# First layer of a four-layer network: gates between the transpositions, 56 stationary columns, halved copies

## The chip, the cores and the metric

The kernel runs on one core of a Trainium2 chip. The core has TensorE (PE; its weight loads are shown as PEld), VectorE (DVE), ScalarE (ACT), GpSimd (POOL) and SyncE (SP), whose queue here issues nearly all DMAs. The metric is the device time of one execution in microseconds. Everything is float32.

## The reference

x has 8 images of 56 x 56 positions with 192 channels. Four layers follow each other, each of the form x = x + layer(group_norm(x)). Only the first is touched:

```python
p = silu(x @ p_w.T + p_b); q = silu(x @ q_w.T + q_b); v = silu(x @ v_w.T + v_b)   # 192 -> 576
a1 = rpe_mlp(positions, t1) * decay; a2 = rpe_mlp(positions, t2) * decay          # 112 x 576
qv = q * v
o1 = toeplitz(qv along w, a1); o2 = toeplitz(qv along h, a2)    # per channel, length 56
out = (p * (o1 + o2)) @ o_w.T + o_b                             # 576 -> 192
```

So for each of 576 channels, each row and each column of the image is convolved with a 56-long two-sided kernel of that channel. The second layer is an outlook attention, the third a windowed gated attention, the fourth a scan in four directions; they begin at about 2.1 ms and end the span.

## The kernel before

An image is kept with channels on partitions: `xa` has the first 128 channels of all 3136 positions, `xb` the last 64, with the image's two halves on the two partition halves. The 576 channels are nine sets of 64 (`NS`), worked in five chunks (`NC`): chunks 0 to 3 have two sets each, chunk 4, the tail, has one. Functions return lists of steps, and `merge(a, b)` calls two lists alternately. TensorE's order is the order in which the program calls (a manual schedule); the other engines' orders are chosen by the scheduler, and each engine works its queue in order.

The work on a chunk:

- `project(xn, c)`, four steps `g`: the q and v products for a band of 7 rows in each half of the image (L294 with `xa`, L301 with `xb`; two PSUM tiles, one for q and one for v; one in the tail), a Silu of each on ScalarE (L310), and the product q * v, written into `qv` twice: as it is (`straight`, L319, VectorE) and with the two image axes exchanged (`across`, L325, mostly GpSimd; in step 3 halved between GpSimd and VectorE). `qv` holds [channel, 56, 120]: one form in columns 0 to 55, the other in 64 to 119, reversed. There is one `qv`, so a chunk's products are written after the transpositions of the chunk before have read it.
- `turn_both(n)`, seven steps of 16 transpositions (L352), which bring positions onto partitions, and two copies of each PSUM tile (L357): rows 0 to 55 (`T2`) by VectorE into `ol`, rows 64 to 119 (`T1`) by ScalarE into `or`. In the tail this is `turn`, with four steps (L371, L378).
- `toeplitz(n)`: the other rows of `ol` and `or` are loaded with the Toeplitz matrices of set n: for image 0 from the small networks' output (L280, and stored to DRAM, L281), later from the stored tables (L275), on SP's queue, after the convolutions of set n - 2 have read their places.
- `convolve(n, ot)`, two steps per set of 32 matmuls (L395): one matmul per channel, contraction over 120 rows (56 of qv and table, a gap, 56 of table and qv), which gives o1 + o2 of that channel as 56 x 56. Two channels go side by side, to output rows 0 to 63 and 64 to 127. The stationary side takes 64 columns, that is the channel's 56 and 8 of the next one, so that the gap rows 56 to 63 of the output are written too. The PSUM tile is copied to `ot` as 120 rows at once: the first step of a set by VectorE (L415), the second by ScalarE (L413); in the tail two copies of 56 rows (L406).
- `post(c // 2, ...)` after chunks 1 and 3, seven groups: the gate p (L436, L443, Silu L450), the transposition of `ot`, with all 120 rows (L461), the product (L470), the output projection (L481, L486) and the addition to `acc` (L422, L424). `post_tail` does this for the tail (L526 to L572, L547 its transposition).

PSUM tiles of the first layer come from `banks()`, four buffers of two banks, handed out in turn; the inputs of the products, `s`, have four buffers too. The main loop takes, for each chunk c:

```python
merge(fill, turns)                      # post step of the chunk before, if any, with the turn
...
ahead = project(xn, c + 1) if two else project(nxt, 0) if more else []
...                                     # convs: the steps of convolve, toeplitz(m + 2) after each set
if c == NC - 2:
    ahead = [f for pair in zip(ahead, convs[0:4]) for f in pair]
    convs = convs[4:]
merge(ahead, beside)                    # the next chunk's projection, with norm steps beside it
for f in convs:
    f()
if c in (1, 3):
    fill = post(c // 2, xn, ot, acc)
```

`fill` is the post step in chunks 2 and 4, the tail's post step in chunk 0 of the next image, and empty in chunks 1 and 3 and in chunk 0 of image 0. `beside` holds, in chunks 0 and 1, the statistics of the finished image (`tell`, with small matmuls L98, table loads for the square root L128 and the VectorE operations L119 to L130 and L608), and in chunk 2 the normalization of the next one (`normalize`: L49 on VectorE, L595 on ScalarE).

Of the kernel before, what the change touches and what calls it, by code (L numbers as in the profile page):

```python
# [17 lines left out]
H = 56  # L18
# [38 lines left out]
def image_dma(queue, dram, xa, xb, store=False):  # L57


    parts = []  # L60
    for at in range(0, HW, HQ // 2):
        cols = slice(at, at + HQ // 2)
        parts.append((xa[0:CP, cols], dram[:, 0, cols]))
        parts.append((xa[CP:CA, cols], dram[0 : CA - CP, 1, cols]))
        h, own = at // HQ, slice(at % HQ, at % HQ + HQ // 2)
        parts.append((xb[h * CB : (h + 1) * CB, own], dram[CA - CP :, 1, cols]))
    for s, d in parts:
        if store:
            queue.dma_start(d, s)
        else:  # L70
            queue.dma_start(s, d)


def sub(ap, *dims):

    return bass.AP(ap.tensor, ap.offset, [list(ap.ap[0]), *(list(d) for d in dims)])
# [59 lines left out]
def layer0(cx, xin, xout, w, consts):  # L136
# [6 lines left out]
    tc, nc = cx.tc, cx.nc  # L143
    B = len(xin)
    NS, DS = 9, 64
    NC = 5
    NP = 112
    T2, T1 = slice(0, H), slice(64, 64 + H)
    cx.open(B)
    cx.between = ExitStack()  # L150
    with ExitStack() as es:
        gn = GroupNormSplit(cx, cx.between, w["gmat"])
        cp = es.enter_context(tc.tile_pool(name="l0c", bufs=1))
# [5 lines left out]
        def banks():  # L159
            return cx.tile(psc, [128, 2, 512], "c")  # L160
# [22 lines left out]
        with ExitStack() as pes:  # L183
# [22 lines left out]
            for t in (1, 2):  # L206
# [13 lines left out]
                for i in range(3):  # L220
                    ps = banks()[0:32, 0, 0:NP]
# [4 lines left out]
                for s in range(NS):  # L226
                    ps = banks()[0:DS, 0, 0:NP]
# [23 lines left out]
        qv = cx.tile(cp, [128, H, 120], "qv")  # L251
        nc.vector.memset(qv[:, :, H:64], 0.0)

        ND = DS * H
# [25 lines left out]

        def project(xn, c):

            n = 7 * H
            tail = c == NC - 1
            js = [2 * c] if tail else [2 * c, 2 * c + 1]

            def step(g):
                pss = [banks() for _ in js]  # L290
                for j, ps in zip(js, pss):
                    for h in range(2):
                        at = h * HQ + g * n
                        nc.tensor.matmul(  # L294
                            ps[:, h, 0:n], wqv[0][:, j, :], xn[0][:, at : at + n],
                            start=True, stop=False,
                        )
                for j, ps in zip(js, pss):
                    for h in range(2):
                        rows = slice(h * CB, (h + 1) * CB)  # L300
                        nc.tensor.matmul(  # L301
                            ps[:, h, 0:n], wqv[1][rows, j, :], xn[1][rows, g * n : (g + 1) * n],
                            start=False, stop=True,
                        )
                ts = []
                for i in range(2):
                    j, ps = js[0 if tail else i], pss[0 if tail else i]
                    rows = slice(i * DS, (i + 1) * DS) if tail else slice(0, 128)
                    t = cx.tile(wk, [128, 2, n], "s")[0 : DS if tail else 128]
                    nc.scalar.activation(t, ps[rows, :, 0:n], AF.Silu, bias=bqv[rows, j : j + 1])  # L310
                    ts.append(t)
                multiply(g, slice(0, DS if tail else 128), ts)

            return [lambda g=g: step(g) for g in range(4)]

        def multiply(g, rows, ts):

            def straight():
                nc.vector.tensor_tensor(  # L319
                    sub(qv[rows, 7 * g :, 64 + H - 1 :], (HH * 120, 2), (120, 7), (-1, H)),  # L320
                    *(t.rearrange("p u (h w) -> p u h w", w=H) for t in ts), ALU.mult,
                )

            def across(eng, u, w0, w1):
                eng.tensor_tensor(  # L325
                    sub(qv[rows, w0:, H - 1 - 7 * g - HH * u :], (120, w1 - w0), (-1, 7)),
                    *(t[:, u].rearrange("p (h w) -> p w h", w=H)[:, w0:w1] for t in ts), ALU.mult,
                )

            if g < 3:  # L330
                straight()
                for u in range(2):
                    across(nc.gpsimd, u, 0, H)
                return

            for i, w in enumerate(((0, HH), (HH, H))):
                across(nc.gpsimd, 0, *w)
                across(nc.vector, 1, *w)
                if i == 0:
                    straight()  # L340
# [40 lines left out]

        def convolve(n, ot):


            s = n % NS
            left, right = pairs[n % 2]
            tail = s == NS - 1

            def step(q):
                ps = banks()  # L390
                for k in range(2):
                    for v in range(8):
                        for u in range(2):
                            d = q * 16 + 8 * k + v + u * 32
                            nc.tensor.matmul(  # L395
                                ps[u * 64 : (u + 1) * 64, k, v * H : (v + 1) * H],
                                left[:, d * H : d * H + 64],
                                right[:, d * H : (d + 1) * H],
                                start=True, stop=True, skip_group_check=True,
                            )  # L400
                if tail:
                    for u, copy in enumerate((nc.vector.tensor_copy, nc.scalar.copy)):
                        d0 = q * 16 + u * 32
                        dst = ot[0:H, :, d0 : d0 + 16].rearrange("p h (k v) -> p h k v", k=2)
                        src = ps[u * 64 : u * 64 + H, :, 0 : 8 * H]
                        copy(dst, src.rearrange("p k (v h) -> p h k v", h=H))  # L406
                    return
                else:
                    d0 = s % 4 * 32 + 16 * q
                    dst = ot[:, d0 : d0 + 16, :].rearrange("p (k v) h -> p k (v h)", k=2)  # L410
                    src = ps[0:120, :, 0 : 8 * H]
                if q % 2:
                    nc.scalar.copy(dst, src)  # L413
                else:
                    nc.vector.tensor_copy(dst, src)  # L415

            return [lambda q=q: step(q) for q in range(2)]

        def add(m, j, x, ps):
# [194 lines left out]
        def merge(a, b):  # L614

            n = max(len(a), len(b))
            for i in range(n):
                for x in (a, b):
                    for f in x[-(-i * len(x) // n) : -(-(i + 1) * len(x) // n)]:
                        f()  # L620
# [7 lines left out]
        xn, nxt = first, None  # L628
        merge(normalize(xn), [])
        for n in range(2):  # L630
            toeplitz(n)
        merge(project(xn, 0), [])
        fill, after, telling = [], None, []
        for b in range(B):
            more = b + 1 < B
            for c in range(NC):
                n = b * NS + 2 * c
                two = c < NC - 1
                turns = turn_both(n) if two else turn(n)
                merge(fill, turns)  # L640
                fill, beside = [], []
                if c == 0:
                    if after is not None:
                        image_dma(nc.sync, xout[b - 1], *after, store=True)
                        beside, telling = tell(b - 1, *after)
                    if more:
                        nxt = load_raw(b + 1)
                if c == 1:
                    acc = new_acc(b)
                    beside = [lambda f=f: f(bank) for f in telling]  # L650
                if c == 2 and more:
                    beside = normalize(nxt)

                if c % 2 == 0:
                    ot = cx.tile(cp, [120, 128, H] if two else [H, H, DS], "ot")
                ahead = project(xn, c + 1) if two else project(nxt, 0) if more else []
                convs = []
                for m in (n, n + 1) if two else (n,):
                    *some, last = convolve(m, ot)
                    convs += some + [lambda m=m, last=last: (last(), toeplitz(m + 2))]  # L660

                if c == NC - 2:
                    ahead = [f for pair in zip(ahead, convs[0:4]) for f in pair]
                    convs = convs[4:]
                merge(ahead, beside)
                for f in convs:
                    f()
                if c in (1, 3):
                    fill = post(c // 2, xn, ot, acc)
            fill, after = post_tail(xn, ot, acc), acc  # L670
            xn = nxt
# [1421 lines left out]
```

## Time and profile before

| | |
|---|---|
| three runs | 4215.12 us median, 4203.36 to 4217.38 |
| profiled execution | 4220.94 us, of which the span of instructions is 4219.1 |
| granted TensorE clock | 0.978 on average |
| busy share of the span | PE 94%, PEld 60%, DVE 55%, ACT 42%, POOL 36% |
| the chain that ended last | PE 76%, DVE 7%, issue 6%, DMA 3%, POOL 3%, ACT 3% |
| convolutions (L395) | 9216 matmul records, 288.7 us busy |
| copies of the turn (L357) | DVE 224 of 1210 ns, ACT 224 of 1008 ns |
| copies of the outcomes | DVE 64 of 1083 ns (L415), ACT 64 of 907 ns (L413) |

A line of a group reads: source line, engine, operation, output<-input, partitions x elements, count, then busy time and the mean of one in ns, then how long the engine was idle before them and what ended that. A float32 matmul leaves two records, each with a weight load. Matmuls overlap, so that the mean of one is longer than the distance from one to the next; for a stream, the length of the whole stream over its records is the number to use. In an order of time the columns are the start in us, the length in us, the engine, the line. "issue" is waiting for nothing that the profile shows.

### The profile page before, as it was taken

To read this page: it belongs to the slowest core of one execution; us is meant where nothing else is said; L and a number is where in the kernel's file an instruction comes from. 1 tells how busy PE (TensorE), PEld (TensorE's weight loads), DVE (VectorE), ACT (ScalarE), POOL (GpSimd) and SP (SyncE) were. 2 spreads that over 40 slices of the span, in tenths; PEclk is the share of its full clock that TensorE was granted. 3 is DMA by queue.
4 is the path that set the end of the run, shared out by engine and by line. 5 is a ranking of instruction groups with operands and counts; after the bars stand their busy time and mean duration, and the time that the engine had idled before them with its cause. 6 is when DMAs were issued, how large, how long until landed. Compare 5 with 4: busy or idle time off the path is not lost.

```text
span 4219.1 us, 106491 instructions
## 1 busy us (share of the span) xinstructions
PE 3948.1 (94%) x46380; PEld 2547.7 (60%) x46380; DVE 2336.7 (55%) x3407; ACT 1785.5 (42%) x2022; POOL 1512.0 (36%) x1302
## 2 busy tenths in 40 slices
PE   6989999999999999999799999799998999998997
PEld 4666656666665666656466666444444555555997
DVE  5536565554656546554544444465656667664664
ACT  2434434334443434444233344233335555554564
POOL 3222232222322222242233333333334444443776
PEclk9999999999999999999899999899999999999999
DMA  6755242242524224242324444565538776663233
GB/s 145 141 107 146 62 116 66 77 97 62 146 62 113 58 70 115 62 105 66 92 66 110 105 101 106 138 185 186 167 130 192 174 171 150 159 144 104 81 110 94
DMA packets 382342, 483.54 MB, mean 115 GB/s; under 512 B 176084, under 2 KB 326724, under 8 KB 380484
## 3 DMA queue, kind: packets, MB, share of 16 engines
q1 hardware_dynamic: 375029, 467.19, 44.0%
q10 hardware_dynamic: 6847, 9.54, 0.8%
q8 instruction: 365, 5.98, 0.6%
q14 instruction: 101, 0.83, 0.1%
HBM read 320.90 MB, written 155.65 MB: 113 GB/s over the span
## 4 chain that ended last, share of the span: by engine, by line
PE 76%; DVE 7%; issue 6%; DMA 3%; POOL 3%; ACT 3%; SPq 1%; ACTq 0%; POOLq 0%; DVEq 0%
PE c L294 9%; PE h L1926 7%; PE v L1418 6%; PE c L395 6%; PE c L301 5%; PE c L481 5%; PE c L436 4%; PE c L948 4%; PE c L461 3%; PE y L983 3%; PE kv L1478 3%; PE c L443 3%; PE c L486 2%; DVE ol L357 2%; PE c L954 2%
## 5 line engine op out<-in xcount | busy, mean ns | idle before, releaser
L325 POOL TENSOR_TENSOR qv<-s,s 128x392 f32<-128x392 f32 (+3 forms) x320 | 567.2, 1793 | 1423.4 <-ACT s L310 1382.5
L310 ACT ACTIVATE s<-c,bqv 128x784 f32<-128x784 f32 (+1 forms) x320 | 278.5, 911 | 383.8 <-PE c L301 224.0
L294 PE MATMUL c<-xa,wqv 128*128 128x392 f32 x1152 | 432.3, 517 | 9.3 <-ACT or L357 6.5
L319 DVE TENSOR_TENSOR qv<-s,s 128x784 f32<-128x784 f32 (+1 forms) x160 | 190.5, 1190 | 267.0 <-ACT s L310 266.9
L357 ACT COPY or<-c 56x1024 f32<-56x1024 f32 x224 | 225.9, 1008 | 256.2 <-DVE ol L357 241.2
L294 PEld LDWEIGHTS c<-xa,wqv 128*128 128x128 f32 x1152 | 210.5, 194 | 177.3 <-issue 42.5
L395 PEld LDWEIGHTS c<-or,ol 120*64 120x64 f32 x9216 | 278.1, 138 | 59.4 <-issue 49.5
L395 PE MATMUL c<-or,ol 120*64 120x56 f32 x9216 | 288.7, 223 | 21.5 <-issue 8.4
L357 DVE COPY ol<-c 56x1024 f32<-56x1024 f32 x224 | 261.6, 1210 | 64.1 <-PE c L352 64.1
L450 ACT ACTIVATE s<-c,bp 128x448 f32<-128x448 f32 x224 | 129.9, 631 | 269.9 <-PE c L443 269.9
L301 PE MATMUL c<-xb,wqv 64*128 64x392 f32 x1152 | 232.9, 518 | 0.0
L1418 PE MATMUL v<-wvb,wa 128*128 128x512 f32 (+1 forms) x400 | 192.9, 615 | 28.7 <-ACT wa L1307 16.8
L1957 POOL TENSOR_TENSOR y<-y,s 128x448 f32<-128x448 f32 x168 | 185.0, 1101 | 91.9 <-ACT s L1936 88.6
L1926 PE MATMUL h<-ringv,am 128*64 128x57 f32 (+1 forms) x4400 | 192.4, 235 | 24.0 <-DVE ringv L1913 17.1
L481 PE MATMUL c<-po,wo 128*128 128x448 f32 x448 | 198.1, 564 | 10.8 <-DVE po L470 10.8
L1429 ACT ACTIVATE vb<-sm 128x1024 f32<-128x1024 f32 (+1 forms) x100 | 103.9, 1040 | 222.2 <-issue 195.6
L436 PE MATMUL c<-xa,wp 128*128 128x224 f32 x896 | 191.3, 356 | 3.6 <-issue 3.6
L1926 PE MATMUL h<-ringh,am 128*64 128x57 f32 (+1 forms) x4400 | 186.5, 232 | 8.4 <-DVE ringh L1932 7.8
L424 DVE TENSOR_TENSOR acca<-c,acca 128x392 f32<-128x392 f32 (+1 forms) x120 | 67.3, 588 | 222.0 <-PE c L486 204.8
L352 PE MATMUL c<-ident,qv 64*120 64x64 f32 x3584 | 143.2, 226 | 44.4 <-ACT or L357 38.9
L1926 PEld LDWEIGHTS h<-ringv,am 128*64 128x64 f32 x4400 | 168.1, 140 | 27.2 <-DVE ringv L1913 18.0
L948 PE MATMUL c<-wv,xc 128*126 128x192 f32 x896 | 175.6, 339 | 0.2 <-ACT v L958 0.2
(230 smaller groups left out, 7681.8 us busy)
## 6 DMA issues: line engine op xcount, KB each, us to landing
or<-tt SPq DMA_DIRECT2D x252, 196.0 KB
ol<-tt SPq DMA_DIRECT2D x252, 196.0 KB
vt<-v SPq DMA_DIRECT2D x56, 672.0 KB
v<-vb SPq DMA_DIRECT2D x96, 384.0 KB
x<-x SPq DMA_DIRECT2D x110, 168.0 KB
x<-x SPq DMA_DIRECT2D x110, 112.0 KB
bs<-bt SPq DMA_DIRECT2D x48, 256.0 KB
bs<-bs SPq DMA_DIRECT2D x54, 224.0 KB
```

What stands on the lines that cost most here:

```text
L294: nc.tensor.matmul(ps[:, h, 0:n], wqv[0][:, j, :], xn[0][:, at : at + n], start=True, stop=False,)
L301: nc.tensor.matmul(ps[:, h, 0:n], wqv[1][rows, j, :], xn[1][rows, g * n : (g + 1) * n], start=False, stop=True,)
L310: nc.scalar.activation(t, ps[rows, :, 0:n], AF.Silu, bias=bqv[rows, j : j + 1])
L319: nc.vector.tensor_tensor(sub(qv[rows, 7 * g :, 64 + H - 1 :], (HH * 120, 2), (120, 7), (-1, H)), *(t.rearrange("p u (h w) -> p u h w", w= ...
L325: eng.tensor_tensor(sub(qv[rows, w0:, H - 1 - 7 * g - HH * u :], (120, w1 - w0), (-1, 7)), *(t[:, u].rearrange("p (h w) -> p w h", w=H)[:, ...
L357: copy(dst[:, :, :, i0 : i0 + 8], view[rows])
L395: nc.tensor.matmul(ps[u * 64 : (u + 1) * 64, k, v * H : (v + 1) * H], left[:, d * H : d * H + 64], right[:, d * H : (d + 1) * H], start=Tr ...
L436: nc.tensor.matmul(out(u, h), wp[0][:, 2 * j + u, :], xn[0][:, at : at + n], start=(u == 0), stop=True, skip_group_check=True,)
L481: nc.tensor.matmul(pa, wo[:, 2 * j + u, 0:CA], pos[u], start=(u == 0), stop=(u == 1))
L948: nc.tensor.matmul(out(i, u), group(i, u), wv[0], start=(u == 0), stop=True, skip_group_check=True,)
L1418: nc.tensor.matmul(out, x[:, at : at + n], wt, start=(k == 0), stop=(k == 1), skip_group_check=True,)
L1926: nc.tensor.matmul(ps[sides[c], y], am[a][:, m * CB : (m + 1) * CB], old[:, x], start=(n < 2), stop=True, skip_group_check=True,)
```

## The change

- In chunks with no `fill`, the first two gates (the matmuls and Silus of `project`) of the next chunk are called between the turn's steps: gate 0 before the first turn step, gate 1 before the fourth. Their products follow after the last turn step, before the rest of the projection. `project` returns pairs (gate, product) for that; `whole` joins them again elsewhere. In chunk 3 the two remaining steps alternate with the first two convolution steps, where four alternated with four.
- The convolutions load 56 stationary columns, no longer 64, and write rows 0 to 55 and 64 to 119.
- The gap rows of the outcome are no longer written by them, so a PSUM tile is copied in two halves of 56 rows: `T2` always by VectorE, `T1` by ScalarE in the first step of a set and by VectorE in the second. Per set that is three VectorE copies and one ScalarE copy, where there was one of each. The second half's copy, if on ScalarE, waits for the first half's.
- `ot` is one tile, `ots`, for the whole layer; its rows 32 to 63 are set to zero once by GpSimd, at the start. The tail uses the same storage in its old form.

The number of matmuls, Silus, products and DMAs stays, and so does the order of DMAs on SP, but that in chunk 1 the two small stores of a finished image's norms (L609, L610) are issued two table loads (L275) later.

```diff
--- before.py
+++ after.py
@@ -251,6 +251,9 @@
         qv = cx.tile(cp, [128, H, 120], "qv")
         nc.vector.memset(qv[:, :, H:64], 0.0)
 
+        ots = cx.tile(cp, [120, 128, H], "ot")
+        nc.gpsimd.memset(ots[32:64], 0.0)
+
 
 
         ND = DS * H
@@ -282,11 +285,14 @@
 
         def project(xn, c):
 
+
             n = 7 * H
             tail = c == NC - 1
             js = [2 * c] if tail else [2 * c, 2 * c + 1]
 
-            def step(g):
+            state = {}
+
+            def gates(g):
                 pss = [banks() for _ in js]
                 for j, ps in zip(js, pss):
                     for h in range(2):
@@ -309,9 +315,12 @@
                     t = cx.tile(wk, [128, 2, n], "s")[0 : DS if tail else 128]
                     nc.scalar.activation(t, ps[rows, :, 0:n], AF.Silu, bias=bqv[rows, j : j + 1])
                     ts.append(t)
-                multiply(g, slice(0, DS if tail else 128), ts)
-
-            return [lambda g=g: step(g) for g in range(4)]
+                state[g] = ts
+
+            def products(g):
+                multiply(g, slice(0, DS if tail else 128), state.pop(g))
+
+            return [(lambda g=g: gates(g), lambda g=g: products(g)) for g in range(4)]
 
         def multiply(g, rows, ts):
 
@@ -381,7 +390,6 @@
 
         def convolve(n, ot):
 
-
             s = n % NS
             left, right = pairs[n % 2]
             tail = s == NS - 1
@@ -393,8 +401,8 @@
                         for u in range(2):
                             d = q * 16 + 8 * k + v + u * 32
                             nc.tensor.matmul(
-                                ps[u * 64 : (u + 1) * 64, k, v * H : (v + 1) * H],
-                                left[:, d * H : d * H + 64],
+                                ps[u * 64 : u * 64 + H, k, v * H : (v + 1) * H],
+                                left[:, d * H : (d + 1) * H],
                                 right[:, d * H : (d + 1) * H],
                                 start=True, stop=True, skip_group_check=True,
                             )
@@ -405,14 +413,12 @@
                         src = ps[u * 64 : u * 64 + H, :, 0 : 8 * H]
                         copy(dst, src.rearrange("p k (v h) -> p h k v", h=H))
                     return
-                else:
-                    d0 = s % 4 * 32 + 16 * q
-                    dst = ot[:, d0 : d0 + 16, :].rearrange("p (k v) h -> p k (v h)", k=2)
-                    src = ps[0:120, :, 0 : 8 * H]
-                if q % 2:
-                    nc.scalar.copy(dst, src)
-                else:
-                    nc.vector.tensor_copy(dst, src)
+                d0 = s % 4 * 32 + 16 * q
+
+                other = nc.vector.tensor_copy if q else nc.scalar.copy
+                for rows, copy in ((T2, nc.vector.tensor_copy), (T1, other)):
+                    dst = ot[rows, d0 : d0 + 16, :].rearrange("p (k v) h -> p k (v h)", k=2)
+                    copy(dst, ps[rows, :, 0 : 8 * H])
 
             return [lambda q=q: step(q) for q in range(2)]
 
@@ -629,7 +635,10 @@
         merge(normalize(xn), [])
         for n in range(2):
             toeplitz(n)
-        merge(project(xn, 0), [])
+        def whole(steps):
+            return [lambda f=f, h=h: (f(), h()) for f, h in steps]
+
+        merge(whole(project(xn, 0)), [])
         fill, after, telling = [], None, []
         for b in range(B):
             more = b + 1 < B
@@ -637,7 +646,13 @@
                 n = b * NS + 2 * c
                 two = c < NC - 1
                 turns = turn_both(n) if two else turn(n)
-                merge(fill, turns)
+
+                ahead = project(xn, c + 1) if two else project(nxt, 0) if more else []
+                early = [] if fill else ahead[0:2]
+                merge(fill + [f for f, _ in early], turns)
+                for _, f in early:
+                    f()
+                ahead = whole(ahead[len(early) :])
                 fill, beside = [], []
                 if c == 0:
                     if after is not None:
@@ -652,16 +667,18 @@
                     beside = normalize(nxt)
 
                 if c % 2 == 0:
-                    ot = cx.tile(cp, [120, 128, H] if two else [H, H, DS], "ot")
-                ahead = project(xn, c + 1) if two else project(nxt, 0) if more else []
+                    ot = ots if two else ots[0:H, 0:DS].rearrange("p d h -> p (d h)").rearrange(
+                        "p (h d) -> p h d", d=DS
+                    )
                 convs = []
                 for m in (n, n + 1) if two else (n,):
                     *some, last = convolve(m, ot)
                     convs += some + [lambda m=m, last=last: (last(), toeplitz(m + 2))]
 
                 if c == NC - 2:
-                    ahead = [f for pair in zip(ahead, convs[0:4]) for f in pair]
-                    convs = convs[4:]
+                    k = len(ahead)
+                    ahead = [f for pair in zip(ahead, convs[0:k]) for f in pair]
+                    convs = convs[k:]
                 merge(ahead, beside)
                 for f in convs:
                     f()
```

## The prediction, made before the changed kernel ran

> **What bounds the kernel now.** I read the page first, then the groups of instructions by shape, then the order of time in image 1 (the eight images repeat it, 250 us each), then the stretches with the clock.
>
> The page and the groups (us busy, mean ns of one, idle before):
>
> ```profile
> PE 3948.1 (94%) x46380; PEld 2547.7 (60%) x46380; DVE 2336.7 (55%) x3407; ACT 1785.5 (42%) x2022; POOL 1512.0 (36%) x1302
> ...
> L395 PE MATMUL c<-or,ol 120*64 120x56 f32 x9216 | 288.7, 223 | 21.5 <-issue 8.4 <-DMA ol<-ed 7.8 <-ACT or L357 4.7
> L395 PEld LDWEIGHTS c<-or,ol 120*64 120x64 f32 x9216 | 278.1, 138 | 59.4 <-issue 49.5 <-ACT or L357 9.6
> L357 DVE COPY ol<-c 56x1024 f32<-56x1024 f32 x224 | 261.6, 1210 | 64.1 <-PE c L352 64.1
> L415 DVE COPY ot<-c 120x896 f32<-120x896 f32 x64 | 69.2, 1083 | 17.5 <-PE c L395 17.4
> L406 DVE COPY ot<-c 56x896 f32<-56x896 f32 x16 | 16.7, 1073 | 1.7 <-PE c L395 1.7
> L406 ACT COPY ot<-c 56x896 f32<-56x896 f32 x16 | 14.5, 903 | 38.2 <-DVE ot L406 37.5
> ```
>
> TensorE is the bound of the span, with little room: 94%. The copy rows carry the rest: a copy of 56 partitions costs what one of 120 costs, and the ScalarE copy of a shared PSUM tile waits for the VectorE copy of the same tile (37.5 us at L406).
>
> The one stage of the first layer in which TensorE isn't full is the turn of a chunk that has nothing to fill it (chunks 1 and 3). Chunk 1 of image 1 in order of time (start, length, engine), up to the post step:
>
> ```profile
> 602.54 7.83 PE L395 MATMUL c<-or,ol 120*64 120x56 f32 x256
> ...
> 607.25 2.27 DVE L415 COPY ot<-c 120x896 f32<-120x896 f32 x2
> ...
> 610.30 2.11 PE L352 MATMUL c<-ident,qv 64*120 64x64 f32 x64
> ...
> 611.03 8.00 DVE L357 COPY ol<-c 56x1024 f32<-56x1024 f32 x7 [1.52 <-PE c L352]
> ...
> 612.28 7.79 ACT L357 COPY or<-c 56x1024 f32<-56x1024 f32 x7 [0.93 <-DVE ol L357]
> ...
> 616.74 4.28 PE L294 MATMUL c<-xa,wqv 128*128 128x392 f32 x8 [0.42 <-ACT or L357]
> ...
> 622.46 0.97 PEld L98 LDWEIGHTS c<-mean,gmat 128*128 128x128 f32 x8 [0.56 <-issue]
> ...
> 637.29 4.57 PEld L395 LDWEIGHTS c<-or,ol 120*64 120x64 f32 x153 [0.56 <-issue]
> ...
> 649.24 1.15 PE L461 MATMUL c<-ident,ot 120*128 120x120 f32 x8
> ```
>
> The seven turn steps go at VectorE's pace, 8.00/7 = 1.14 us each, while TensorE needs 0.5 us for one (2.11 for four); the first gate waits behind them for banks. The same stage as stretches (PE, PEld, DVE, ACT, POOL busy, granted clock, DMA share, GB/s):
>
> ```profile
> 610.00:616.00 6.00, 4.17 (x122) 3.71 (x119) 4.97 (x5) 4.26 (x5) 0.00 (x0) 1.00 0.90 241
> 616.00:622.00 6.00, 5.58 (x24) 2.94 (x22) 3.03 (x3) 3.71 (x4) 0.00 (x0) 0.72 0.99 241
> 622.00:628.00 6.00, 6.00 (x29) 3.32 (x26) 4.31 (x7) 2.48 (x3) 3.10 (x2) 1.00 0.44 92
> 628.00:634.00 6.00, 6.00 (x27) 3.40 (x26) 2.04 (x4) 3.39 (x5) 4.41 (x3) 1.00 0.00 0
> ```
>
> After the thin 6 us the clock falls to 0.72: 0.28 x 6 = 1.7 us lost. And chunk 3, in the chain that ended last:
>
> ```profile
> 722.20 8.02 DVE ol L357 x7
> ...
> 730.24 1.02 ACT or L357
> ...
> 731.30 2.15 PE c L395 x64
> ```
>
> Here the convolutions wait for the last turn copy on ScalarE.
>
> **Part 1: 56 stationary columns.** Two records (one in each half of the array) take 2 x 7.6/256 = 59 ns. The load sets that: the 128-column loads of L98, with one moving column, come every 0.97/8 = 121 ns, twice the 59 of 64 columns. By columns, 56 give 52 ns: 4608 pairs x 7 = 32 us of TensorE, 0.95 us a chunk. No row has 56; the bounds are 0 (a strip loads whole) and 1.1 us a chunk (matching 57/64 of everything). I take 0.95, because 64 and 128 lie on one line through it.
>
> **Part 2: copies in halves.** A chunk of two convolutions has four steps. Before: two VectorE copies (1.08) and two ScalarE (0.91). After: six on VectorE and two on ScalarE that wait behind one. VectorE gets 4 x 64/2 = 128 more copies, 137 us in all, 4.3 us a chunk of its 32; back to back they start about every 1.0 us (seven copies of L357, 1.21 each, take 8.00: each starts 0.08 before the last has ended; 1.08 - 0.08). TensorE reads the copied tile only in the post step (L461), so in chunks 0 and 2 the cost falls on the turn copies queued behind on VectorE, in chunks 1 and 3 on L461.
>
> The rows above have 56x896 at 1073 ns on VectorE and 903 on ScalarE; had ScalarE taken every second half, VectorE would have four copies a chunk and be done 2 us sooner. The Trainium skill (TensorEngine Tiling (Array Packing), PSUM Bottleneck) says to use both ScalarE and VectorE to empty PSUM, which speaks against "mostly VectorE": by it, 2 us a chunk before the post step are given away, some 30 us over 16 chunks.
>
> **Part 3: two gates inside the turn, chunk 0 to chunk 2.** Count from s = 602.54, the start of chunk 0's convolutions. TensorE ends them at s+6.7. VectorE does the last products until s+4.7, as now, then six copies, until s+10.8. Gate 0 (4.35 from one gate's start to the next's, as at 589.49 and 593.84) runs s+6.7 to 11.1, over that backlog; three turn steps until 12.7; gate 1 until 17.1; four more until 19.1. VectorE (seven copies, 8 us) is inside this; ScalarE (seven copies, four Silus of 0.86) has copied step 3 at s+20.0, which gives gate 2 its bank. Gate 2 ends at s+24.4, where before gate 1 ended at 25.2 with an L98 group of 1.0 in between: a gate further. The convolutions of chunk 1 start at s+30.9 and not 637.29 = s+34.75. The products of the early gates can't write qv until the last turn step has read it (19.1); GpSimd then needs 3.1 to 3.9 a gate, and the Silus of gates 2 and 3, which reuse its inputs' buffers, come later than that (24.0, 29.1). Tables: the DMA is idle from 628 on (0.00), wanted at 633.4: covered by some 5 us. On SP only the two small norm stores change places, two table loads back; the loads behind them wait for L608 until s+37.8 and are wanted in chunk 2, some 70 us later.
>
> Then the evacuation: last Silu s+30.9, products 3.3, first copy 35.2, the four small norm operations queued behind it on VectorE (L129 to L608, 2.5), five copies: 42.8. L461 runs at s+42.9, before at 649.24 = s+46.7. **Gain 3.8.**
>
> **Chunk 2 to chunk 4.** Count from s = 713.36. The first copy and the last products end at s+6.5, as now; five copies, 11.6. The turn copies begin there, not at 722.20 = s+8.84. ScalarE's seven turn copies plus the four early Silus (0.92 each) end at s+22.0, so that the convolutions start at s+22.0, before at 731.30 = s+17.9; but three gates of 2.2 are done by then, before one. GpSimd frees the buffers for Silu 2 at 22.4; Silu 24.2, product 25.2, first copy 26.2, ScalarE's half, a new wait with the last Silu queued behind it, 27.2, last Silu 29.1, products 32.4, five copies 37.5. L461 at s+37.6; before it started at 750.13 = s+36.8 (36.3 to 36.8 over the images). **Loss 1.2.** The tail (chunk 4) keeps its copies, and L547 behind them: nothing.
>
> **Image 0.** The turn of chunk 0 has nothing to fill it either, and there TensorE waits from 68.0 to 70.55 for the last products: gate 0 fits there, 7 us gained; 4 more in chunk 1 (no norm operations); in chunk 3 a table load of 14.65 us (ol<-ed) is the bound, so that its loss vanishes and about 5 are kept. **Gain 16.** The 6.1 us memset on GpSimd (the row of L259 is 6086 ns) lies before the first table load, which waits until 42 us for the small networks; without that cover it would cost 6.
>
> **Sum.** 7 x (3.8 - 1.2) + 16 = 34 us. From this comes what the clock takes back: TensorE now waits 2 to 3 us before L461 in both post chunks and runs a thin chunk 3; up to three half-clock stretches an image at 1.7 us, of which today's one or so is already in the rows: 0 to 24 us, I take 8, since chunk 1, where the row shows it, becomes dense. The profiled execution (4220.94, span 4219.1) gives 4221 - 26 = 4195. It lies 5.8 above the median of the runs, 4215.12: on that scale 4189.
>
> The row has 4.17 of 6 us busy and then 0.72. The Trainium skill (TensorE: Matmul & The Clock Gate, Why this matters for your kernels) asks for no idle gap over about 3 us between bursts: by that, both waits before L461 just miss it or just hit it, and if all hit, the sum is 34 - 24 = 10 us of gain.
>
> **Rivals.**
> - VectorE becomes the bound (0.22). For: in chunks 1 and 3 L461 now hangs on a VectorE chain of 9 to 12 us. If its copies keep their row's 1.08 and products and copies don't overlap with GpSimd as well, chunk 3 loses its turn delay (2.7) and five copies (5.4) in full: 8.1 x 8 = 65 against 3.8 x 7 + 11 = 38 gained: 27 slower, 4242. (11 is image 0's 16 less the 5 of its chunk 3.) It decides once L461 in chunk 4 slips by more than 38/8 = 4.7 us. Against: VectorE is 55% busy and the following post steps leave it half idle.
> - The gains cancel (0.16): columns save nothing (7 us of what I count) and the clock takes 20: about 4208.
> - The pairs no longer run side by side, as 56 isn't half an array (0.02): 4608 x 45 ns = 207 us slower. Against: L352 pairs row halves with 120 columns.
>
> **How the numbers follow.** The forecast has 0.60, 4189 (own range 4156 to 4203). A measurement of this kernel can tell about 0.3%, 12.6 us, from no change. Faster 0.60, same 0.16, slower 0.24. The low end has no clock loss and all 32 us of part 1 on the path instead of 7: 4215 - 34 - 25 = 4156. The high end reaches most of the first rival, 4238; above it lie some 0.12 with the last rival, below some 0.04.
>
> **What would show it.** Right: L395 with 56 columns at about 52 ns a pair; in chunk 1 no gap between turn steps and full clock at its end; L461 in chunk 2 some 43 us after chunk 0's first convolution and, in chunk 4, 38 us after chunk 2's, released by VectorE's ot copy; chunk 3's convolutions still released by ScalarE's turn copy. Wrong: L395 unchanged at 59; L461 in chunk 4 later than 41; new half-clock stretches in each post chunk.

## The result, and the profile after

| | before | after |
|---|---|---|
| median | 4214.37 us (4203.36 to 4219.64) | 4231.8 us (4221.64 to 4238.97) |
| ratio | | 1.0041, 95% interval 1.0031 to 1.0051 |
| span of the profiled execution | 4219.1 us | 4231.5 us |
| granted clock over the span | 0.978 | 0.973 |

The change makes the kernel 0.4% slower. The forecast was 4189; the time lies inside the range of 4156 to 4238, but on the other side of no change. (The image that the prediction counts from, called image 1 there, is the third one. It is called image 2 here: images are counted from 0.)

First the page after, and its groups by shape:

```profile
PE 3931.1 (93%) x46380; PEld 2530.6 (60%) x46380; DVE 2507.8 (59%) x3535; ACT 1781.8 (42%) x2022; POOL 1529.6 (36%) x1303
...
L403 PE MATMUL c<-or,ol 120*56 120x56 f32 x9216 | 252.8, 216 | 13.6 <-issue 6.0 <-DMA ol<-ed 5.5 <-ACT or L366 2.0
L421 DVE COPY ot<-c 56x896 f32<-56x896 f32 x192 | 204.9, 1083 | 6.4 <-PE c L403 4.6
L467 PE MATMUL c<-ident,ot 120*128 120x120 f32 x896 | 133.3, 294 | 25.7 <-ACT s L456 14.7 <-DVE ot L421 11.0
L421 ACT COPY ot<-c 56x896 f32<-56x896 f32 x64 | 57.7, 901 | 237.4 <-DVE ot L421 237.2
L328 DVE TENSOR_TENSOR qv<-s,s 64x784 f32<-64x784 f32 x32 | 56.5, 1788 | 7.2 <-ACT s L316 7.2
```

TensorE has 36 us less to do in the convolutions (L403 252.8, L395 before 288.7), and VectorE has the 128 copies more, 204.9 us where L415 had 69.2. L467 is the transposition of the outcome (L461 before). It never waited before:

```profile
L461 PE MATMUL c<-ident,ot 120*128 120x120 f32 x896 | 128.7, 287 | 0.0
```

Now it waits 25.7 us in all, for VectorE's copies and for a Silu on ScalarE. The ScalarE row of L421 says why ScalarE is late: its half copies stand 237.2 us behind the VectorE half of the same tile, with whatever is queued after them.

Chunk 3 of image 2, in order of time (start, length, engine; its convolutions of chunk 2 begin at s = 709.32):

```profile
715.98 5.40 DVE L421 COPY ot<-c 56x896 f32<-56x896 f32 x5
...
719.31 0.90 ACT L421 COPY ot<-c 56x896 f32<-56x896 f32 x1 [5.71 <-DVE ot L421]
...
729.07 11.72 POOL L334 TENSOR_TENSOR qv<-s,s 64x392 f32<-64x392 f32 x6 [13.41 <-PE c L361]
...
731.23 6.40 DVE L328 TENSOR_TENSOR qv<-s,s 64x784 f32<-64x784 f32 x3
732.39 1.80 PEld L403 LDWEIGHTS c<-or,ol 120*56 120x56 f32 x64 [1.34 <-ACT or L366]
...
737.56 1.07 DVE L421 COPY ot<-c 56x896 f32<-56x896 f32 x1
...
738.66 0.90 ACT L421 COPY ot<-c 56x896 f32<-56x896 f32 x1 [3.62 <-DVE ot L421]
...
739.59 1.85 ACT L316 ACTIVATE s<-c,bqv 64x784 f32<-64x784 f32 x2
...
744.60 5.40 DVE L421 COPY ot<-c 56x896 f32<-56x896 f32 x5
...
747.93 0.90 ACT L421 COPY ot<-c 56x896 f32<-56x896 f32 x1 [6.49 <-DVE ot L421]
748.85 1.16 ACT L456 ACTIVATE s<-c,bp 128x448 f32<-128x448 f32 x2
...
750.15 1.83 PE L467 MATMUL c<-ident,ot 120*128 120x120 f32 x8 [2.09 <-ACT s L456]
```

From 731 to 750 one chain runs through VectorE and ScalarE: three products that take 6.40 us, a copy, ScalarE's half copy and last Silus, the last products, five copies. The fifth of these and the Silu of the gate behind ScalarE's half copy (L456) both end at 750.0, and L467 starts. The chain that ended last runs through the same instructions:

```profile
731.30 3.81 DVE qv L328 x2
...
735.30 2.33 DVE qv L328
737.63 1.01 DVE ot L421
...
738.66 0.91 ACT ot L421
...
739.59 0.92 ACT s L316
```

The same stage of image 3 in stretches (PE, PEld, DVE, ACT, POOL busy, granted clock, DMA share, GB/s), just ahead of L467 at 1002.98 and behind it:

```profile
996.00:1002.00 6.00, 2.77 (x28) 2.03 (x26) 5.94 (x7) 1.22 (x2) 1.11 (x1) 0.99 0.91 239
1002.00:1008.00 6.00, 5.02 (x18) 4.29 (x20) 3.20 (x4) 1.85 (x3) 0.00 (x0) 0.50 0.15 39
```

TensorE is busy 2.77 us of six, and then runs at half its clock for six.

To see where the time went, cut the first layer at six events of each image: the first convolution of chunks 0, 2 and 4, the first transposition of an outcome in chunks 2 and 4 (L461, after L467), and the first of the tail (L547, after L553). The sums are worked out from the two traces.

| stage | before | after | forecast of the difference | measured |
|---|---|---|---|---|
| start to the first convolution | 96.5 | 90.5 | -7 | -6.0 |
| chunk 0 to L461 in chunk 2, image 0 | 44.4 | 48.5 | -4 | +4.1 |
| the same, images 1 to 7, sum | 327.1 | 305.7 | -26.6 | -21.4 |
| chunk 2 to L461 in chunk 4, image 0 | 46.3 | 42.5 | -5 | -3.8 |
| the same, images 1 to 7, sum | 254.9 | 279.7 | +8.4 | +24.8 |
| L461 in chunk 4 to chunk 4, sum | 476.8 | 492.1 | (clock) | +15.3 |
| tail to the next image, sum | 231.3 | 238.5 | (clock) | +7.2 |
| other stages | | | 0 | -1.3 |
| first layer, to the last tail | 2048.4 | 2067.2 | -26 with 8 for the clock | +18.8 |

Of the 18.8 us the later layers, which are the same work, give back 6: their instructions run 19 us late at the end of the first layer and 14 us late at 2650 us. The span differs by 12.4.

### The profile page after: what moved, and what is told of

Read it like the earlier page. It is cut to its first block, busy times and chain, and to the rows that moved or that the text cites. A ratio compares the mean times of both kernels' runs of the same rounds, so it can differ in the third digit from the quotient of the medians.

```text
span 4231.5 us, 106744 instructions
## 1 busy us (share of the span) xinstructions
PE 3931.1 (93%) x46380; PEld 2530.6 (60%) x46380; DVE 2507.8 (59%) x3535; ACT 1781.8 (42%) x2022; POOL 1529.6 (36%) x1303
## 4 chain that ended last, share of the span: by engine, by line
PE 66%; DVE 13%; issue 6%; ACT 5%; POOL 4%; DMA 3%; SPq 2%; ACTq 0%; POOLq 0%; DVEq 0%
PE c L300 7%; PE v L1435 6%; PE h L1943 6%; PE c L487 5%; PE c L965 4%; PE c L442 4%; PE c L307 3%; PE c L467 3%; PE y L1000 3%; DVE ot L421 3%; PE kv L1495 3%; PE c L492 2%; PE c L449 2%; DVE qv L328 2%; PE c L971 2%
## 5 line engine op out<-in xcount | busy, mean ns | idle before, releaser
L334 POOL TENSOR_TENSOR qv<-s,s 128x392 f32<-128x392 f32 (+3 forms) x320 | 579.8, 1838 | 1417.2 <-ACT s L316 1172.9
L328 DVE TENSOR_TENSOR qv<-s,s 128x784 f32<-128x784 f32 (+1 forms) x160 | 227.4, 1430 | 157.7 <-ACT s L316 157.4
L403 PEld LDWEIGHTS c<-or,ol 120*56 120x56 f32 x9216 | 245.5, 133 | 38.0 <-issue 33.2
L403 PE MATMUL c<-or,ol 120*56 120x56 f32 x9216 | 252.8, 216 | 13.6 <-issue 6.0
L456 ACT ACTIVATE s<-c,bp 128x448 f32<-128x448 f32 x224 | 129.7, 630 | 260.9 <-PE c L449 260.6
L421 DVE COPY ot<-c 56x896 f32<-56x896 f32 x192 | 204.9, 1083 | 6.4 <-PE c L403 4.6
L1943 PEld LDWEIGHTS h<-ringv,am 128*64 128x64 f32 x4400 | 168.0, 140 | 26.2 <-DVE ringv L1930 16.9
```

What stands on the lines that cost most here:

```text
L328: nc.vector.tensor_tensor(sub(qv[rows, 7 * g :, 64 + H - 1 :], (HH * 120, 2), (120, 7), (-1, H)), *(t.rearrange("p u (h w) -> p u h w", w= ...
L334: eng.tensor_tensor(sub(qv[rows, w0:, H - 1 - 7 * g - HH * u :], (120, w1 - w0), (-1, 7)), *(t[:, u].rearrange("p (h w) -> p w h", w=H)[:, ...
L403: nc.tensor.matmul(ps[u * 64 : u * 64 + H, k, v * H : (v + 1) * H], left[:, d * H : (d + 1) * H], right[:, d * H : (d + 1) * H], start=Tru ...
L421: copy(dst, ps[rows, :, 0 : 8 * H])
L1943: nc.tensor.matmul(ps[sides[c], y], am[a][:, m * CB : (m + 1) * CB], old[:, x], start=(n < 2), stop=True, skip_group_check=True,)
```

## The experiments

**Theory Q**: VectorE's longer queue is the cost, by its half copies and by the ScalarE halves that wait behind them; early gates gain. **Theory G**: the early gates in chunk 3 are the cost. **Theory C**: the thin stretches and the lowered clock are. Each ratio is against the kernel before on the same chip, with its 95% interval. Runs 1 to 4 share a chip, so do 5 to 8 and 9 to 12. One kernel measured on two chips gave 0.9854 and 0.9882 (runs 1 and 11), so some 0.3% between runs of different chips shows nothing by itself; the first layer's own count repeats better (2006.4 and 2005.8 there, 1998.8 and 1998.7 in runs 7 and 12). "First layer" is the start of the last tail's first transposition in the run's profile (before 2048.4 us, after 2067.2).

**1. Early gates alone**, on the kernel before: 64 columns, whole copies.

```
 left[:, d * H : d * H + 64]                      # as before
 copy of ps[0:120]: VectorE first step, ScalarE second   # as before
+early = [] if fill else ahead[0:2]               # as in the change
```

> The kernel before with the early gates alone (64 stationary columns, whole copies of 120 rows, one by VectorE and one by ScalarE per set). Theory Q (the cost of the change is the longer VectorE queue: half copies, and ScalarE halves that wait behind them): about 4 us gained per image from chunk 0 to chunk 2, little lost in chunk 3, so 4180 to 4195. Theory G (the cost is calling two gates early in chunk 3, where ScalarE's Silus stand among the turn's copies and the products fall together): 3 us lost per image in chunk 3 as in the changed kernel, which leaves some 4200 to 4210. Theory C (what is gained goes to the half-clock stretches of TensorE): near 4215, with some 25 half-clock stretches in the first layer.

Measured: 0.9854 (0.9841 to 0.9868), 1.5% faster, more than any of the three theories gave (theory Q's 4180 to 4195 us are 0.992 to 0.995 of the kernel before); first layer 2006.4. Chunk 3 gains too: from chunk 2 to L467 it takes 34.6 us in images 1 to 7, before 36.3 to 36.8. Theory G falls: the gates are what gains. Chunk 3 of image 2 in order of time (s = 701.78; in this kernel L325 and L331 are the products, L401 the convolutions):

```profile
719.63 14.74 POOL L331 TENSOR_TENSOR qv<-s,s 64x392 f32<-64x392 f32 x8 [11.51 <-PE c L358]
...
721.34 6.85 DVE L325 TENSOR_TENSOR qv<-s,s 64x784 f32<-64x784 f32 x3
...
722.55 2.15 PE L401 MATMUL c<-or,ol 120*64 120x56 f32 x64 [0.30 <-ACT or L363]
...
727.00 5.81 PE L401 MATMUL c<-or,ol 120*64 120x56 f32 x192
...
733.54 1.07 DVE L421 COPY ot<-c 120x896 f32<-120x896 f32 x1
...
736.35 0.92 PE L467 MATMUL c<-ident,ot 120*128 120x120 f32 x6
```

The products are as slow here as in the change (6.85 us for three), but one copy, not five, follows the last product, and it is done 1.7 us before L467, which waits for nothing. So slow products alone don't hold L467 up; the copies queued behind them do.

**2. 56 columns and half copies, no early gates.**

```
-early = [] if fill else ahead[0:2]
+early = []
```

> The changed kernel with no early gates: 56 columns and half copies stay. Theory Q: the turn of chunks 1 and 3 waits for two more VectorE copies (about 2 us each), and the transposition of the outcome for one or two more (1 to 2 us), less 0.95 us a chunk from the columns: 3 to 5 us slower per image than the kernel before, 4240 to 4255. Theory G: the columns gain and the copies hide: 4200 to 4215. Theory C: as Q or G, plus 1.7 us for each added half-clock stretch.

Measured: 1.0212 (1.0198 to 1.0226), some 90 us slower, over twice what theory Q asked for. First layer 2145.0: 23 us more than before in the stage from chunk 0, 45 in the stage from chunk 2, and 18 between L467 and chunk 4, with half-clock stretches of 222 us in all in the first layer (before 51, after 106).

**3. The second half always on ScalarE**, four half copies a chunk on each engine.

```
-other = nc.vector.tensor_copy if q else nc.scalar.copy
+other = nc.scalar.copy
```

> The changed kernel with the second half always copied by ScalarE: four half copies a chunk on each engine, not six and two. Theory Q: VectorE is done about 2 us sooner in chunks 0 and 2 and about 1 us sooner in chunks 1 and 3: 2 to 4 us per image, 4200 to 4218. Theory G: within 8 us of the changed kernel's 4232, or slower, as ScalarE is the engine that chunk 3 waits for.

Measured: 0.9968 (0.9955 to 0.9980). Two copies fewer on VectorE in each chunk and two more on ScalarE give 0.7%, about 31 us, against the changed kernel, as theory Q says (24 us by the first layer's count, 2042.7).

**4. Early gates not in chunk 3.**

```
-early = [] if fill else ahead[0:2]
+early = ahead[0:2] if not fill and c != NC - 2 else []
```

> The changed kernel with early gates only in chunk 1 and in chunk 0 of image 0; chunk 3 alternates four gates with four convolution steps as before. Theory Q: the backlog of VectorE stays in chunk 3, and without early gates nothing fills TensorE there meanwhile: 4225 to 4245. Theory G: chunk 3 goes back to the time of the kernel before while chunk 1 keeps its 3.8 us per image: 4195 to 4208.

Measured: 1.0074 (1.0060 to 1.0088): slower than the change (first layer 2082.5), as theory Q says. From chunk 2 to L467 it takes 41.1 to 43.3 us in images 1 to 7; with the gates 39.4 to 40.8. So the early gates in chunk 3 hide a part of the half copies' cost there.

**5. Early gates, whole copies, 56 columns for one channel of a pair.** Whole copies need the gap rows written, so that the channel in rows 0 to 55 keeps 64.

```
-left[:, d * H : d * H + 64]
+left[:, d * H : d * H + (H if u else 64)]
```

> The early gates with whole copies, and 56 stationary columns only for the channel in output rows 64 to 119; the one in rows 0 to 55 keeps 64, so that the gap rows are still written and a tile can be copied whole. If the two loads of a pair count one after the other, a pair takes 55 to 56 ns (half the way from 59 to 52), 16 us of TensorE, and TensorE is full in nearly all of these stages: 0.985 of the kernel before goes to 0.981 to 0.983. If the longer of two loads sets the pair: 59 ns and 0.985.

Measured: 0.9895 (0.9880 to 0.9910), no gain over the early gates alone, and above both expected figures; on the third chip the gates alone gave 0.9882. The two loads of a pair are not a sum. A chunk's 256 records, in order of time (L401), still take 7.67 us, as with 64 and 64 (7.68 in run 1), where 56 and 56 take 6.83 in the changed kernel:

```profile
619.35 7.67 PE L401 MATMUL c<-or,ol 120*64 120x56 f32 x256
```

A pair takes the time of its wider member.

**6. Half copies alone**, with 64 columns and no early gates.

```
-left[:, d * H : (d + 1) * H]
+left[:, d * H : d * H + 64]
-early = [] if fill else ahead[0:2]
+early = []
```

> The half copies alone: the kernel before with its 64 columns, no early gates, T2 by VectorE and T1 by ScalarE or VectorE as in the change. Theory Q (the copies are the whole cost): 1.021 of the kernel before, as with 56 columns, or up to 1.028, by the 32 us of TensorE that the columns save. Rival (the shorter loads have a cost of their own): under 1.015.

Measured: 1.0200 (1.0183 to 1.0217). With 56 columns it was 1.0212: the intervals overlap, and the first layer ends at 2143.4 and 2145.0. The copies bring the whole cost, and without the early gates the columns are worth nothing that these runs can see. Much of the cost goes through the clock: half of TensorE's busy time in half-clock stretches, an estimate of what they take, is 82 us in this first layer and 22 before, some 60 of the 95 us by which it is longer. The rest is idle time of TensorE (167 us, before 131).

**7. Both halves of a tile on one engine**, four and four, so that none crosses.

```
-for rows, copy in ((T2, nc.vector.tensor_copy), (T1, other)):
+copy = nc.scalar.copy if q else nc.vector.tensor_copy
+for rows in (T2, T1):
```

> The changed kernel with both halves of the first step's tile copied by VectorE and both of the second step's by ScalarE: four each, as in the run with T1 on ScalarE (0.997), but no ScalarE copy waits for a VectorE copy of its own tile. If the number on VectorE is the cost, 0.997 again (0.994 to 0.999). If the wait of ScalarE behind VectorE costs as well, 0.985 to 0.992.

Measured: 0.9896 (0.9881 to 0.9912), first layer 1998.8. Against run 3 the same counts on the same engines, without the crossing, are another 0.7% faster, so the wait of ScalarE behind VectorE costs as well. The waits that answer to those of the change are small or of another kind:

```profile
L421 DVE COPY ot<-c 56x896 f32<-56x896 f32 x128 | 139.1, 1087 | 6.3 <-PE c L403 4.3
L467 PE MATMUL c<-ident,ot 120*128 120x120 f32 x896 | 128.5, 286 | 4.9 <-DVE ot L421 4.9
L421 ACT COPY ot<-c 56x896 f32<-56x896 f32 x128 | 115.2, 900 | 103.0 <-PE c L403 102.0
```

L467 waits 4.9 us where it waited 25.7. ScalarE's half copies now wait for TensorE (102.0 of 103.0 us, 128 copies), where 64 waited 237.2 for VectorE.

**8. The first post gate of chunk 4 done twice**, to fill TensorE ahead of L467 in the changed kernel (its lines are one later here, L468).

```
 def gate(g):
+    for _ in range(2 if j == 1 and g == 0 else 1):
         ... (the gate's 8 matmuls, 16 records)
```

> The changed kernel with the 16 matmuls of the first gate in the post step of chunk 4 done twice, with the same result: 2.8 us more of TensorE where it waits 2.4 and 2.1 us before the first transposition of the outcome. Theory C (thin stretches lower the clock, and that is the loss from this transposition to chunk 4): the half-clock stretch there goes, that stage is back at 61.8 us from 63 to 64.6, and the whole at 0.999 to 1.001 of the kernel before. Theory Q alone: TensorE only waits less, 1.003 to 1.007.

Measured: 1.0010 (1.0000 to 1.0021), first layer 2055.2: 2.8 us more work an image, and it is 12 us shorter. From L468 to chunk 4 it takes 61.8 us in five of images 0 to 6 (63.4 and 63.1 in the two others) and 44.3 in the last, 479.7 in sum, where the change has 492.1 and the kernel before 476.8. Image 3, the same two stretches:

```profile
998.00:1004.00 6.00, 4.83 (x44) 4.11 (x41) 5.91 (x7) 2.06 (x3) 0.00 (x0) 1.00 0.89 222
1004.00:1010.00 6.00, 6.00 (x37) 4.00 (x36) 1.99 (x4) 2.17 (x3) 0.00 (x0) 1.00 0.05 13
```

TensorE is busy 4.83 us of the first six, and the clock stays at 1.00. So theory C holds for this stage, as a consequence of the wait: L468 itself is hardly earlier (38.6 to 40.8 us after chunk 2's first convolution in images 1 to 7).

**9. Six and two without crossing.** Three tiles of a chunk go to VectorE and the last to ScalarE.

```
-copy = nc.scalar.copy if q else nc.vector.tensor_copy
+copy = nc.scalar.copy if q and s % 2 else nc.vector.tensor_copy
```

> The changed kernel with six half copies a chunk on VectorE and two on ScalarE, as in the change, but both halves of a tile on one engine: three tiles to VectorE, the last of the chunk to ScalarE. So far: six and two with crossing 1.0041, four and four with crossing 0.997, four and four without 0.990. If number and crossing are two costs that add (0.7% each): 0.995 to 0.999. If the crossing is most of it: 0.989 to 0.993. If the number on VectorE is: 1.000 to 1.004.

Measured: 1.0023 (1.0012 to 1.0035). With the runs before, a table of two by two, all with early gates and 56 columns:

| half copies a chunk | T2 and T1 of a tile on two engines | on one engine |
|---|---|---|
| six VectorE, two ScalarE | 1.0041 (the change) | 1.0023 |
| four and four | 0.9968 | 0.9896, 0.9891 |

The number on VectorE is the greater part (0.7 and 1.3%). The crossing costs 0.7% with four and four. With six and two its cost isn't shown: 0.2% lies within what two chips differ by, and the first layers (2067.2 with crossing, 2066.0 without) differ by 1 us. By the same count four and four take 2042.7 and 1998.8, so the two remedies together (68 us) give far more than each alone (24 and 1).

**10. No early gates, four and four on one engine.**

```
-early = [] if fill else ahead[0:2]
+early = []
```

> No early gates, 56 columns, both halves of a tile on one engine, four and four. With no early gates and the change's own copies it was 1.021. If the copies cost the same with and without early gates (1.5% between the change and four and four without crossing): about 1.006. If the early gates also hide copies: 1.008 to 1.015.

Measured: 1.0042 (1.0029 to 1.0054), a little below the lowest of the expected figures: the copies as the change has them cost 1.7% against these without early gates (1.0212 to 1.0042), and 1.5% with them (1.0041 to 0.9896). The early gates hide little of it in sum, as far as runs on different chips can tell.

**11 and 12. Early gates alone, and run 7, beside each other.**

> The early gates alone, with 64 columns and whole copies, once more, to stand beside the next kernel on one chip: 0.984 to 0.988. In the profile of its first run the first layer ended 8 us later than in that of the next kernel, so if the columns are worth something once TensorE is full, it is the slower of the two by up to 8 us.

> Early gates, 56 columns, both halves of a tile on one engine (four and four), once more, beside the run of the early gates alone: 0.984 to 0.990. If the half copies, twice as many as whole ones, cost what the columns save, within 4 us of the early gates alone.

Measured: 0.9882 (0.9868 to 0.9896) and 0.9891 (0.9874 to 0.9908). Side by side the two can't be told apart. Both beat both kernels: 1.2 to 1.5% below the kernel before over the two runs of the one, 1.0 to 1.1% for the other. In the first layer's own count run 12 is 7 us ahead (1998.7 against 2005.8), so that 56 columns save a little where TensorE is full: 41.1 to 42.7 us from chunk 0 to L467 in images 1 to 7, against 42.7 to 43.8. In chunk 3 the halves take 0.6 back (35.2 against 34.6).

What 56 columns with whole copies would give is open: the gap rows of the copied tile are then not written.

## Why the prediction was wrong

**Part 1, columns: right in size.** 256 records take 6.61 us from first to last start, 52 ns a pair. Run 6 beside run 2 shows that little of it lay on the path, as the prediction said of 7 us in 32.

**Part 2, copies: right in count, mis-sized in place.** 204.9 - 69.2 = 135.7 us more on VectorE (137 forecast). The prediction booked them stage by stage as covered, but for 1.2 us an image in chunk 3 and a part of chunk 1. Alone they cost 2.0%, some 85 us, of the 137. Its remark that four and four would give some 30 us was right in run 3 (0.7%, 31 us): here rule and run agree, and the Trainium skill's rule (TensorEngine Tiling (Array Packing), PSUM Bottleneck: empty PSUM with both engines) spoke against this change. Run 7 shows that it also matters whether an engine gets whole tiles.

**Part 3, chunk 0 to chunk 2: right.** Forecast 42.9 us; measured 42.6 to 43.1 in five of images 1 to 7 (44.2 and 47.7 in the two others, where TensorE also stands still for 1.3 and 0.8 us within the convolutions of chunk 0; in the second it then waits 2.2 us for ScalarE's half copy, with a half-clock stretch behind it). The way there fits too: the convolutions of chunk 1 were forecast at s+30.9 and start at s+31.2 in image 2, and L467 is released by VectorE's copy. Chunk 1's turn runs at full clock.

**Chunk 2 to chunk 4: the step that failed.** Forecast s+37.6, measured s+39.4 to s+40.8, so that the loss is 24.8 us over seven images and not 8.4. One term was too small: the products of steps 0 to 2 on VectorE were put at 1.0 us each, from rows in which VectorE starts ahead of GpSimd. Here GpSimd is already running (from 729.07) when VectorE comes free from its copies (731.23), and in image 2 each product takes 6.40/3 = 2.13 us (1.0 to 2.4 over the images). The first copy after them starts at s+28.2 and ends at s+29.3; the forecast had it end at 26.2. What hangs on that copy keeps the forecast's lengths and comes 3 us late: ScalarE's half copy, which the prediction did count as a new wait, the last Silus (their end s+32.1 and not 29.1), the products (3.2), the five copies (5.40). The trace before had the price:

```profile
L319 DVE TENSOR_TENSOR qv<-s,s 64x784 f32<-64x784 f32 x32 | 36.7, 1147 | 72.7 <-ACT s L310 72.7
...
742.17 0.97 DVE L319 TENSOR_TENSOR qv<-s,s 64x784 f32<-64x784 f32 x1 [3.39 <-ACT s L310]
742.28 3.88 POOL L325 TENSOR_TENSOR qv<-s,s 64x392 f32<-64x392 f32 x2 [0.51 <-ACT s L310]
...
746.66 2.81 POOL L325 TENSOR_TENSOR qv<-s,s 64x196 f32<-64x196 f32 x2 [0.50 <-ACT s L310]
747.01 1.69 DVE L319 TENSOR_TENSOR qv<-s,s 64x784 f32<-64x784 f32 x1
```

The mean of 1147 ns hides two kinds: 24 products of 967 ns that start ahead of GpSimd's, and 8 of 1684 that start while GpSimd runs.

On these products the Trainium skill (SBUF — State Buffer, SBUF: two separate sides) has a mechanism: a VectorE instruction with two SBUF inputs and a GpSimd one that reads SBUF share a port pair, which the one that starts first holds to its end. The rows agree: 967 ns for the one that is first, 2361 on average where GpSimd is in the middle of its row of products (run 1). No run takes GpSimd's products away, so that it is the cause is not shown by an experiment.

**The clock: the other mis-sized term.** Taken at 8 us. The half-clock stretches of the first layer went from 51 to 106 us, and the two stages that have nothing else new lost 15.3 + 7.2 = 22.5 us, near the upper bound of 24. (The estimate of run 6, half of TensorE's busy time at half clock, gives 48 us for the whole first layer and 22 before.) Run 8 returns 12.4 of the 15.3 by filling TensorE. The prediction cited a rule of the Trainium skill (TensorE: Matmul & The Clock Gate, Why this matters for your kernels), which asks for no idle gap over about 3 us. In image 3 the gaps were 2.1 and 2.1 us with 1.1 us of work between them, and the clock fell to 0.50. The measurement decides: a thin stretch is enough without such a gap.

**Image 0: 16 forecast, 5.7 measured.** The first convolution came 6 us earlier, where 7 were forecast. Chunk 1 gave 4 back where 4 more were expected: TensorE waits 2.0 us for the backlog of half copies, 2.6 us for a turn copy that the statistics of the next image had got ahead of (VectorE works on them from 107.6 to 112.1 us), and stands still for 2.5 us in the middle of the last convolution step, for nothing that the profile names (0.3 us at the same place before). None of the three was tried alone. But run 1, with whole copies, has the last two at the same places (2.5 and 2.7 us) and only 0.2 us at the first: the first belongs to the half copies, the two others don't. What the last one is stays open.

**The sum.** Forecast -26 in the first layer, measured +18.8. Of the 45 between them 16 are chunk 3, 14.5 the clock, 10 image 0 and 5 chunk 1. Of the rivals the first, VectorE as the bound, was right in kind. Its point of decision was not reached: L467 in chunk 4 slipped by 3.5 us an image and not 4.7, and the clock's 22 us did the rest. The time lies inside the stated range because its high end was reckoned from this rival, not from the sum. What the prediction lacked was the cost of each part alone: -1.5% and +2.0%, of which it saw the small difference through stages worked by hand.

## What to carry to other kernels

- When a change joins a gain with a cost, price the cost alone first. Here the gates gain 1.2 to 1.5% and the copies that came with them, six on VectorE and two on ScalarE, take all of it: a copy of half the partitions costs as much as a whole one (1083 and 1083 ns, 901 and 907), so halving a copy doubles its time on the engine. Shared out four and four in whole tiles, the same half copies leave the gain standing (0.9891, run 12).
- Give each engine whole PSUM tiles. A half that waits behind the other engine's half holds up everything queued after it (run 7 against run 3).
- Take a duration from rows with the same neighbours, and not from a group's mean: a product of two SBUF tiles took 0.97 us where it started ahead of GpSimd's products and up to 2.4 where GpSimd was running.

## What the runs showed of the hardware

- Two convolution matmuls side by side in the two halves of the array, their weight loads included, take the time of the wider one: 59 ns a pair for 64 and 64 stationary columns, 52 for 56 and 56, and again 59 for 64 and 56.
- The clock fell to half after six microseconds with 2.77 busy and no gap over 2.2 us; with 4.83 busy, in the same place of run 8, it did not.
- More work on TensorE (2.8 us an image) made the first layer 12 us shorter (run 8).
